# Deformable convolution: adding the bilinear corners pairwise on VectorE, through PSUM, ahead of the transposes

## The chip, the core and the metric

The kernel runs on one core of a Trainium2 chip. The metric is device time in microseconds for one launch on the whole input (four images). A core has a TensorE for matrix products and transposes, VectorE and ScalarE for element-wise work, GpSimd, which here also issues the gathers, SyncE for other transfers, and the memories SBUF and PSUM. In the profile they are PE (with PEld, its weight loads), DVE, ACT, POOL and SP.

## The reference, cut to what matters

Four layers act on x of shape 4 x 56 x 56 x 128: a window-attention block, a state-space block (selective scan), a deformable 3 x 3 convolution and a second window-attention block; each is applied to a group-normalised x and added to it. The change lies in the third layer:

```python
offsets = lax.conv_general_dilated(x, offset_w, ...) + offset_b       # 9 taps x (dy, dx)
py = row + ky + dy;  px = col + kx + dx
y0, x0 = floor(py), floor(px);  wy, wx = py - y0, px - x0
val = gather(y0i, x0i) * ((1 - wy) * (1 - wx))[..., None] + gather(y0i, x0i + 1) * ((1 - wy) * wx)[..., None] \
    + gather(y0i + 1, x0i) * (wy * (1 - wx))[..., None] + gather(y0i + 1, x0i + 1) * (wy * wx)[..., None]
out = jnp.einsum('bhwkc,kcf->bhwf', val, kernel.reshape(KK, C, F)) + bias
```

For each of the 3136 positions of an image and each of 9 taps, four corner vectors of 128 channels are weighted and summed, and the 9 sums are multiplied with a 128 x 128 matrix each.

## The kernel before, in words

The images go one after the other through the four layers. The residual image x stays in SBUF, channels on the partitions.

`deform` first normalises x, writes into a table in DRAM, for each position, the four corner vectors of its cell side by side (512 floats a row), computes the offsets, the row numbers (`idx`) and the four corner weights (`wts`, which lie in PSUM, two banks). Then comes the part that the change touches, in a schedule written out by hand: each engine executes its own instructions in the order in which the loop below names them, and waits only for data and for free buffers.

The 3136 positions are 28 tiles of 112 positions (`QB`), four tiles (`nq`) to a column block of 448 (`CH`), seven blocks to an image. For each tile t:

- `gather(t)` (L1298): nine indirect DMAs, one per tap, issued by GpSimd; each fetches 112 table rows, positions on the partitions, into the buffer `g` of the tile. There are four such buffers, so the gathers of tile t wait until the transposes of tile t-4 have released theirs.
- `weigh(t)` (L1307): three VectorE products in place, each over three taps and four corners, 1,536 elements per partition. I call three taps of a tile a third.
- `turn(t)` (L1318): the patches must be turned so that channels lie on the partitions. For each tap, TensorE transposes the four corner blocks one after the other into the same PSUM columns and adds them there, which also sums the four corners. Three taps fill a PSUM tile (`pvt`, four buffers), which ScalarE copies to SBUF (L1319) into `turned`. That is 36 transposes and three copies per tile, 4032 and 336 in all.
- After `turn` of tile 4(c+1), or at the very end for the last block, `product(c)` (L1325): nine products of 128 x 128 by 128 x 448 summed in PSUM (`pdo`, 18 matmul records), then on VectorE the addition of bias and residual (L1327) and the statistics of the next normalisation (L115).

The order matters in one place: VectorE meets the addition of block c after the weighing of tile 4(c+1) and before that of tile 4(c+1)+1, so it stands there until TensorE has the product. The next layer starts when the last addition and its statistics are done, since its normalisation needs the whole image.

Of the kernel before, what the change touches and what calls it, by code (L numbers as in the profile page):

```python
# [10 lines left out]
F32 = mybir.dt.float32  # L11
# [3 lines left out]
ALU = mybir.AluOpType  # L15
# [4 lines left out]
P = 128  # L20
# [15 lines left out]
QB = 112  # L36
NTB = L // QB
# [12 lines left out]
KK = 9  # L50
# [28 lines left out]
class _Net:  # L79
# [1123 lines left out]
    def deform(self, b, x):  # L1203
# [3 lines left out]
        nc, tc, w = self.nc, self.tc, self.w["L2"]  # L1207
# [3 lines left out]
        with tc.tile_pool(name="df", bufs=1) as s1, tc.tile_pool(name="df_ps", bufs=1, space=PSUM) as s1x, tc.manual_schedule():  # L1211
# [3 lines left out]
            wts = [wps[:QB, i, :nw].rearrange("q (n k) -> q n k", k=4) for i in range(2)]  # L1215
            with tc.tile_pool(name="dc", bufs=1) as sb, tc.tile_pool(name="dc_ps", bufs=6, space=PSUM) as ps:
# [7 lines left out]
                for c in range(NCK):  # L1224
                    cols = slice(c * CH, (c + 1) * CH)
                    self.gn_apply(xg[:, cols], x[:, cols], gn)
                    pt = bank("pgt")
                    for i in range(nq):
                        t = c * nq + i
                        nc.tensor.transpose(pt[:QB, i * P : (i + 1) * P], xg[:, t * QB : (t + 1) * QB], self.ident)  # L1230
                    nc.scalar.copy(gt[:, c * nq : (c + 1) * nq, :].rearrange("q t c -> q (t c)"), pt[:QB, :])
                    if c in (3, NCK - 1):
                        ts = slice(0 if c == 3 else 4 * nq, (c + 1) * nq)
                        for k in range(4):
                            for r in range(2):

                                y = r + 1 - k // 2
# [9 lines left out]
                for g in range(2):  # L1247
                    n = min(4, NCK - 4 * g)
                    pf = bank("pf")
                    for k in range(KK):  # L1250
                        ky, kx = k // 3, k % 3
                        for j in range(n):
                            c = 4 * g + j
                            nc.tensor.matmul(
                                pf[32 * j : 32 * j + 32, :CH].rearrange("p (h w) -> p h w", w=HW),
                                lhsT=w["offset_w"][:, k * 32 : (k + 1) * 32],
                                rhs=gp[:, 8 * c + ky : 8 * c + ky + 8, kx : kx + HW],
                                start=(k == 0),
                                stop=(k == KK - 1),
                            )  # L1260
                    nc.scalar.activation(of[: 32 * n, g, :], pf[: 32 * n, :CH], AF.Identity, bias=w["offset_b"][: 32 * n, :])
                for g in range(2):
                    n = min(4, NCK - 4 * g)
                    pt = bank("pof")
# [27 lines left out]
            with tc.tile_pool(name="dg", bufs=2) as sb, tc.tile_pool(name="dg_ps", bufs=2, space=PSUM) as ps:  # L1292
                patch, turned = {}, {}

                def gather(t):
                    patch[t] = sb.tile([QB, KK, 4 * P], F32, tag="g", name="g", bufs=4)
                    for k in range(KK):
                        nc.gpsimd.indirect_dma_start(  # L1298
                            out=patch[t][:, k], out_offset=None, in_=tab[:, :],
                            in_offset=bass.IndirectOffsetOnAxis(ap=idx[:, t * KK + k : t * KK + k + 1], axis=0),  # L1300
                        )

                def weigh(t):
                    g = patch[t].rearrange("q k (s c) -> q (k s) c", s=4)
                    wv = wts[2 * t // NTB][:, t % (NTB // 2) * KK : (t % (NTB // 2) + 1) * KK, :].rearrange("q k s -> q (k s)")
                    for k in range(0, 4 * KK, 12):
                        nc.vector.tensor_tensor(g[:, k : k + 12], g[:, k : k + 12], wv[:, k : k + 12, None].to_broadcast([QB, 12, P]), ALU.mult)  # L1307

                def turn(t):
                    c, i = divmod(t, nq)  # L1310
                    if i == 0:
                        turned[c] = sb.tile([P, KK, CH], F32, tag="vt", name="vt")
                    g = patch.pop(t)
                    for k in range(0, KK, 3):
                        pt = ps.tile([P, 3, QB], F32, tag="tr", name="pvt", bufs=4)
                        for m in range(3):
                            for s in range(4):
                                nc.tensor.matmul(pt[:, m, :], lhsT=g[:, k + m, s * P : (s + 1) * P], rhs=self.ident[:QB, :QB], start=(s == 0), stop=(s == 3), is_transpose=True)  # L1318
                        nc.scalar.copy(turned[c][:, k : k + 3, i * QB : (i + 1) * QB], pt)  # L1319

                def product(c):
                    vt = turned.pop(c)
                    po = ps.tile([P, 512], F32, tag="y", name="pdo")
                    for k in range(KK):
                        nc.tensor.matmul(po[:, :CH], lhsT=w["kernel"][:, k * P : (k + 1) * P], rhs=vt[:, k, :], start=(k == 0), stop=(k == KK - 1))  # L1325
                    cols = slice(c * CH, (c + 1) * CH)
                    nc.vector.scalar_tensor_tensor(x[:, cols], po[:, :CH], w["bias"], x[:, cols], ALU.add, ALU.add)  # L1327
                    self.stats(x, c)

                for t in range(NTB + 1):  # L1330
                    if t < NTB:
                        gather(t)
                        weigh(t)
                        turn(t)

                    if t >= nq and t % nq == 0 and t < NTB:
                        product(t // nq - 1)
                product(NCK - 1)

    def finish(self, b, x, cols):  # L1340
# [108 lines left out]
```

## Time and profile before

| | |
|---|---|
| median of three runs | 13576.5 us (13573.9 to 13580.56) |
| the profiled execution's own time | 13561.7 us |
| its span, first to last instruction | 13559.6 us |
| busy: PE, PEld | 12015.1 us (89%), 7682.4 us (57%) |
| busy: DVE, ACT, POOL | 9310.6 us (69%), 7569.9 us (56%), 9553.4 us (70%) |
| first stage, first gather to last addition | 381.30 us (2157.09 to 2538.39) |
| busy in it: PE, PEld, DVE, ACT, POOL | 221.72, 168.99, 149.65, 35.46, 235.71 us |
| in it: granted TensorE clock, share of the DMA engines | 0.69, 0.54 |

The span lies in one profiled execution; the 2.1 us between it and that execution's time lie around it. The shares of the whole span mix four layers with different limits, so the rows of the stage count here. There are four such stages, one per image. A line of the profile names the kernel's line, the engine, the operation, the output and input by the program's names and the count; "idle before" is how long the engine had stood, and "<-" what ended it. "issue" means that the profile shows nothing it waited for; "remote" that it can't name the releaser.

### The profile page before, as it was taken

The page shows a single profiled execution, that of the slowest core. Times are in us where ns is not written, and L with a number is a line of the kernel's source. Part 1 is how long each engine was busy: PE and PEld are TensorE (multiplying, and loading weights), DVE is VectorE, ACT ScalarE, POOL GpSimd, SP SyncE. Part 2 cuts the span into 40 slices and gives each one's busy share as a digit, 9 for nine tenths or more (in the row PEclk, how much of TensorE's full clock was granted, in tenths as well). Part 3 has the DMA queues.
Part 4 walks back from the last instruction along what each step waited for, and adds up shares of the span by engine and source line. Part 5 has one row for each costly group of instructions (what it writes and reads, how often), then busy time and mean ns, then how long its engine had stood idle before and what let it go on. Part 6 is the DMA issues. An engine that isn't in the chain of part 4 may idle for free. (4 is left out here: it accounts for less than half of the span.)

```text
span 13559.6 us, 223295 instructions
## 1 busy us (share of the span) xinstructions
PE 12015.1 (89%) x88500; PEld 7682.4 (57%) x88500; DVE 9310.6 (69%) x11503; ACT 7569.9 (56%) x19306; POOL 9553.4 (70%) x6660
## 2 busy tenths in 40 slices
PE   8989995799998999579999899957999989995799
PEld 4448883544544888354444488845444448884544
DVE  6649993565665999356467499944656659994564
ACT  5567761356556776135655677613565567761356
POOL 4849994477484999448748499943874849994386
PEclk9999997899999999789999899978999999997899
DMA  2000004200000000420000000042000000004200
GB/s 97 1 13 5 4 4 123 68 1 8 4 1 13 5 4 4 126 65 1 8 4 1 13 5 4 4 126 64 1 9 3 1 13 5 4 4 128 62 1 6
DMA packets 181196, 344.93 MB, mean 25 GB/s; under 512 B 20104, under 2 KB 101416, under 8 KB 180024
## 3 DMA queue, kind: packets, MB, share of 16 engines
q0 software_dynamic: 80640, 231.28, 6.1%
q1 hardware_dynamic: 99224, 97.83, 2.3%
q8 instruction: 700, 11.47, 0.4%
q14 instruction: 344, 2.82, 0.1%
q10 hardware_dynamic: 288, 1.53, 0.0%
HBM read 256.04 MB, written 74.52 MB: 24 GB/s over the span
## 5 line engine op out<-in xcount | busy, mean ns | idle before, releaser
L545 POOL TENSOR_TENSOR es<-es,e 128x896 f32<-128x896 f32 x1824 | 3768.0, 2089 | 483.2 <-ACT e L539 440.5
L347 DVE TENSOR_REDUCE mx<-pm 128x1 f32<-128x512 f32 (+2 forms) x4928 | 3060.0, 671 | 1321.4 <-PE pm L346 715.8
L539 ACT ACTIVATE e<-pst 128x448 f32<-128x448 f32 (+1 forms) x5600 | 2675.6, 544 | 1993.4 <-PE pst L537 1405.7
L1056 DVE TENSOR_TENSOR_SCAN hs<-da,dbu 128x928 f32<-128x928 f32 x1792 | 3633.0, 2070 | 53.4 <-ACT dbu L1049 29.0
L1065 POOL TENSOR_TENSOR hs<-hs,cb 128x896 f32<-128x896 f32 x1792 | 3463.4, 1943 | 26.0 <-ACT carry L1060 20.4
L346 PE MATMUL pm<-ks,qs 32*128 32x512 f32 (+1 forms) x9856 | 2886.2, 634 | 14.1 <-DVE nm L363 8.5
L537 PE MATMUL pst<-qs,ks 32*128 32x448 f32 x11200 | 2680.9, 547 | 0.0
L1074 PE MATMUL yt<-w_C,hs 128*116 128x128 f32 x14336 | 1865.5, 273 | 1.1 <-POOL hs L1065 1.1
L532 PE MATMUL pst<-nm,sel 32*128 32x448 f32 x5600 | 1615.5, 612 | 0.0
L1074 PEld LDWEIGHTS yt<-w_C,hs 128*116 128x116 f32 x14336 | 1570.3, 135 | 2.1 <-POOL hs L1065 2.1
L1038 PE MATMUL dbu<-dgb,ut 112*128 112x224 f32 x7168 | 1257.5, 298 | 270.0 <-DVE hs L1056 269.9
L1298 POOL DMA_INDIRECT g<-tab,idx x1008 | 940.2, 933 | 626.9 <-issue 432.5
L561 PE MATMUL po<-e,va 128*32 128x448 f32 (+1 forms) x11200 | 1350.8, 551 | 0.0
L346 PEld LDWEIGHTS pm<-ks,qs 32*128 32x128 f32 x9856 | 909.7, 185 | 741.7 <-DVE mx L347 592.1
L1318 PE MATMUL pvt<-w_C,g 112*128 112x112 f32 x4032 | 652.8, 321 | 710.0 <-issue 603.9
L1038 PEld LDWEIGHTS dbu<-dgb,ut 112*128 112x128 f32 x7168 | 944.4, 192 | 535.5 <-DVE hs L1056 525.6
L992 ACT ACTIVATE da<-dl,A 128x112 f32<-128x112 f32 x3584 | 1194.5, 383 | 0.1
L537 PEld LDWEIGHTS pst<-qs,ks 32*128 32x128 f32 x11200 | 1101.3, 184 | 105.6 <-issue 19.2
L1318 PEld LDWEIGHTS pvt<-w_C,g 112*128 112x128 f32 x4032 | 555.3, 178 | 817.0 <-issue 795.8
L532 PEld LDWEIGHTS pst<-nm,sel 32*128 32x128 f32 x5600 | 558.1, 184 | 751.2 <-DVE mx L347 378.6
L1319 ACT COPY vt<-pvt 128x336 f32<-128x336 f32 x336 | 142.0, 440 | 1413.2 <-remote 921.8
L1060 ACT COPY carry<-hs 128x32 f32<-128x32 f32 x1792 | 397.6, 222 | 624.4 <-DVE hs L1056 616.3
(228 smaller groups left out, 15590.6 us busy)
## 6 DMA issues: line engine op xcount, KB each, us to landing
tab<-zero SPq DMA_DIRECT2D x4, 6728.0 KB
g<-tab,idx POOLq DMA_INDIRECT x1008
tab<-gt SPq DMA_DIRECT2D x32, 448.0 KB
dl_d<-dl SPq DMA_DIRECT2D x28, 448.0 KB
dl<-dl_d SPq DMA_DIRECT2D x56, 224.0 KB
tab<-gt SPq DMA_DIRECT2D x32, 336.0 KB
out_dram<-x SPq DMA_DIRECT2D x28, 224.0 KB
x<-in_x_dram SPq DMA_DIRECT2D x21, 224.0 KB
```

The source lines that it names most:

```text
L346: nc.tensor.matmul(pm[:, :m], lhsT=qs[head(h), q.start : q.start + P], rhs=ks[head(h), keys], start=True, stop=True)
L347: nc.vector.tensor_reduce(mx[:n, h, kc : kc + 1], pm[:n, :m], AX.X, ALU.max)
L532: nc.tensor.matmul(t[:, :CH], lhsT=self.sel[head(h), :], rhs=nm[head(h), part(qc)], start=True, stop=False)
L537: nc.tensor.matmul(t[:, :CH], lhsT=ks[head(h), k * KB : (k + 1) * KB], rhs=qs[head(h), part(qc)], start=False, stop=True)
L539: nc.scalar.activation(e[:nk, j, :], t[:nk, :CH], AF.Exp, scale=SCALE)
L545: nc.gpsimd.tensor_tensor(s, es[g - 1, p][:nk] if k == 1 else s, e[:nk], ALU.add)
L561: nc.tensor.matmul(m["po"][head(h), :CH], lhsT=va[:nk, k, head(h)], rhs=src(h)[:nk], start=(k == 0), stop=(k == NKB - 1))
L1038: nc.tensor.matmul(pu[:, 8 * h : 8 * h + 8, 2 + tb * TB : 2 + (tb + 1) * TB], lhsT=made[g]["ut", 2 * r + tb][:, d, :], rhs=made["r", g // ...
L1056: nc.vector.tensor_tensor_scan(flat(pairs[u // 2][:, d % 2]), flat(made[g]["da"][:, r]), flat(banks.pop(u)), 0.0, ALU.mult, ALU.add)
L1065: nc.gpsimd.tensor_tensor(hs, hs, made["r", g // 2]["cb"][:, :, r * HW : (r + 1) * HW], ALU.mult)
L1074: nc.tensor.matmul(sums[q][:YR, e * P : (e + 1) * P], lhsT=hs[:, n, :], rhs=self.ident, start=(n == 0), stop=(n == NST // 2 - 1), is_trans ...
L1318: nc.tensor.matmul(pt[:, m, :], lhsT=g[:, k + m, s * P : (s + 1) * P], rhs=self.ident[:QB, :QB], start=(s == 0), stop=(s == 3), is_transpo ...
```

## The change

The corners lie in the order (top left, top right, bottom left, bottom right) as four blocks of 128 channels. `weigh` now takes each third in three instructions instead of one: it multiplies the last two corners (`far`) with their weights into a new PSUM tile `pa` (two banks, one buffer), multiplies the first two in place, and adds `far` to them in place. Two blocks remain per tap, so `turn` transposes and sums two instead of four: 18 transposes a tile. To make room in PSUM, the transposing tile `pvt` has three buffers instead of four, and the product's tile `pdo` one instead of two. Each `far` product waits for the sum before it, whose input it overwrites, and each sum for the product just before it. Gathers, copies, products and their order are as they were.

```diff
                 def weigh(t):
-                    g = patch[t].rearrange("q k (s c) -> q (k s) c", s=4)
-                    wv = wts[2 * t // NTB][:, t % (NTB // 2) * KK : (t % (NTB // 2) + 1) * KK, :].rearrange("q k s -> q (k s)")
-                    for k in range(0, 4 * KK, 12):
-                        nc.vector.tensor_tensor(g[:, k : k + 12], g[:, k : k + 12], wv[:, k : k + 12, None].to_broadcast([QB, 12, P]), ALU.mult)
+
+                    g = patch[t].rearrange("q k (s c) -> q k s c", s=4)
+                    wv = wts[2 * t // NTB][:, t % (NTB // 2) * KK : (t % (NTB // 2) + 1) * KK, :, None].to_broadcast([QB, KK, 4, P])
+                    for k in range(0, KK, 3):
+                        ks = slice(k, k + 3)
+                        pa = ps.tile([P, 2, 512], F32, tag="pa", name="pa", bufs=1)
+                        far = pa[:QB].rearrange("q a b -> q (a b)")[:, : 6 * P].rearrange("q (k s c) -> q k s c", k=3, s=2)
+                        nc.vector.tensor_tensor(far, g[:, ks, 2:, :], wv[:, ks, 2:, :], ALU.mult)
+                        nc.vector.tensor_tensor(g[:, ks, :2, :], g[:, ks, :2, :], wv[:, ks, :2, :], ALU.mult)
+                        nc.vector.tensor_tensor(g[:, ks, :2, :], g[:, ks, :2, :], far, ALU.add)
 
                 def turn(t):
...
                     for k in range(0, KK, 3):
-                        pt = ps.tile([P, 3, QB], F32, tag="tr", name="pvt", bufs=4)
+                        pt = ps.tile([P, 3, QB], F32, tag="tr", name="pvt", bufs=3)
                         for m in range(3):
-                            for s in range(4):
-                                nc.tensor.matmul(pt[:, m, :], lhsT=g[:, k + m, s * P : (s + 1) * P], rhs=self.ident[:QB, :QB], start=(s == 0), stop=(s == 3), is_transpose=True)
+                            for s in range(2):
+                                nc.tensor.matmul(pt[:, m, :], lhsT=g[:, k + m, s * P : (s + 1) * P], rhs=self.ident[:QB, :QB], start=(s == 0), stop=(s == 1), is_transpose=True)
                         nc.scalar.copy(turned[c][:, k : k + 3, i * QB : (i + 1) * QB], pt)
 
                 def product(c):
                     vt = turned.pop(c)
-                    po = ps.tile([P, 512], F32, tag="y", name="pdo")
+                    po = ps.tile([P, 512], F32, tag="y", name="pdo", bufs=1)
```

## The prediction

> **What bounds the kernel now.** I read the groups of the page first, then the waits and the timeline of one deformable stage, the only place the diff touches. In the groups, columns are busy time and mean, then idle time before and what ended it:
>
> ```profile
> L1298 POOL DMA_INDIRECT g<-tab,idx x1008 | 940.2, 933 | 626.9 <-issue 432.5
> L1318 PE MATMUL pvt<-w_C,g 112*128 112x112 f32 x4032 | 652.8, 321 | 710.0 <-issue 603.9
> L1319 ACT COPY vt<-pvt 128x336 f32<-128x336 f32 x336 | 142.0, 440 | 1413.2 <-remote 921.8
> ```
>
> No engine is full in this stage: TensorE idles as long as it works, waiting for nothing the profile names. The timeline of VectorE shows the shape of the stage, first image:
>
> ```profile
> 2255.38 0.69 DVE L1327 SCALAR_TENSOR_TENSOR x<-pdo,w_L,x 128x448 f32<-128x448 f32 x1 [38.44 <-PE pdo L1325]
> 2256.10 0.63 DVE L115 BATCH_NORM_STATS2 gn_st<-x 128x6 f32<-128x448 f32 x1
> 2256.65 20.05 DVE L1307 TENSOR_TENSOR g<-g,wt 112x1536 f32<-112x1536 f32 x12
> 2307.51 0.68 DVE L1327 SCALAR_TENSOR_TENSOR x<-pdo,w_L,x 128x448 f32<-128x448 f32 x1 [30.81 <-PE pdo L1325]
> ...
> 2513.13 0.68 DVE L1327 SCALAR_TENSOR_TENSOR x<-pdo,w_L,x 128x448 f32<-128x448 f32 x1 [30.19 <-PE pdo L1325]
> 2513.85 0.63 DVE L115 BATCH_NORM_STATS2 gn_st<-x 128x6 f32<-128x448 f32 x1
> 2514.39 15.05 DVE L1307 TENSOR_TENSOR g<-g,wt 112x1536 f32<-112x1536 f32 x9
> 2537.71 0.68 DVE L1327 SCALAR_TENSOR_TENSOR x<-pdo,w_L,x 128x448 f32<-128x448 f32 x1 [8.26 <-PE pdo L1325]
> ```
>
> From the first gather at 2157.09 the stage is an opening of 98.3 us to the first addition, five rounds of four tiles each (257.75 us, 51.5 each), a tail of 24.6 and the last addition of 0.7: 381.3 us. In every round VectorE weighs 12 thirds of a tile in 20 us and then stands about 30 us until the product is there. So VectorE has room, and the round is set elsewhere. GpSimd's timeline:
>
> ```profile
> 2239.39 0.93 POOL L1298 DMA_INDIRECT g<-tab,idx  x1 [0.30 <-issue]
> 2240.63 0.93 POOL L1298 DMA_INDIRECT g<-tab,idx  x1 [0.30 <-issue]
> 2245.32 0.93 POOL L1298 DMA_INDIRECT g<-tab,idx  x1 [3.76 <-remote]
> ```
>
> A gather costs 1.237 us, the 36 of a round 44.5 us. Twice a round one waits about 3.5 us longer: 44.5 + 2 x 3.5 = 51.5, the whole round. What it waits for is a buffer that TensorE has not released. TensorE and ScalarE in the first gathers:
>
> ```profile
> 2191.30 0.35 PE L1318 MATMUL pvt<-w_C,g 112*128 112x112 f32 x1 [1.65 <-issue]
> 2194.09 0.35 PE L1318 MATMUL pvt<-w_C,g 112*128 112x112 f32 x1 [2.44 <-issue]
> 2196.89 0.35 PE L1318 MATMUL pvt<-w_C,g 112*128 112x112 f32 x1 [2.45 <-issue]
> ```
> ```profile
> 2182.91 0.44 ACT L1319 COPY vt<-pvt 128x336 f32<-128x336 f32 x1 [7.57 <-PE pvt L1318]
> 2212.30 0.44 ACT L1319 COPY vt<-pvt 128x336 f32<-128x336 f32 x1 [28.95 <-remote]
> 2219.37 1.34 ACT L1319 COPY vt<-pvt 128x336 f32<-128x336 f32 x3 [6.63 <-remote]
> ```
>
> The transposes for the copy at 2212.30 are drawn at 2180 to 2182.6; their copy came 30 us later, just after the last gather before the long pause (2211.72). While gathers flow, TensorE finishes a first batch promptly and then trickles: 12 matmuls and 12 weight loads from 2190 to 2219 us, 0.86 instructions per us. In a pause it catches up within about 4.4 us. I don't know what holds it, only that it goes with gathers in flight.
>
> **What the skill says.** The Trainium skill, Perfetto Trace Analysis, "Summary: the profiler window per engine type": a TensorE end is estimated. The 30 us between drawn end and copy agree, so I date completions by the copies. PSUM — Partial Sum Buffer, "Engine vs sequencer instructions": TensorE's queue is 64 deep and matmuls complete in order; the trace agrees in kind, late completions holding all behind them. SBUF — State Buffer, "Who interferes with whom": a VectorE instruction with at most one SBUF input doesn't contend with GpSimd. The gathers keep 1.237 us while VectorE weighs; all three new operations keep one input in PSUM, so I charge them nothing there.
>
> **The change, step by step.**
> VectorE. A third was one product of 1,536 elements, 1748 ns: 148 above 1536/0.96. VectorE: DVE Perf Modes, "The TRN2 errata", gives (N+151)/0.96, so 1757, which agrees. The new 768-element product I put at 800 + 148 = 948 ns. In a burst, thirds follow each other every 1664 ns, 84 less than one lasts. Now the far product waits for the previous sum, the near one waits for nothing new, and the sum waits for the near product, at 30 ns per wait (addition end to statistics above): 948 + 864 + 30 + 948 + 30 = 2.82 us a third, not 1.66. No row writes 768 elements to PSUM or reads both kinds so; bounds 2.6 and 3.4. Behind the far product's wait queue all later thirds, the addition and the statistics; TensorE waits for them, then GpSimd through the buffers.
> What hides it: 12 thirds take 33.8 us; with 1.3 for addition and statistics, 0.7 for the last turn, 7 to 9 for the product and 0.6 to the next addition, VectorE's loop is 43.4 to 45.4 us, about GpSimd's 44.5. The cover is just enough in the rounds; at 3.4 us a third it is gone. In the tail there is none: nine thirds cost 25.4 instead of 15.05, less 0.7 for half a turn: 24.6 + 10.3 - 0.7 = 34.2 us.
> TensorE. A third falls from 12 pairs and a semaphore wait (25 instructions) to 6 pairs and one (13). A round falls from 12 x 25 + 36 for the product = 336 to 192. Two pauses cleared 336, 168 each, of which 22 trickled in 25.7 us and 146 came in a burst. Then 192 = 146 n + 0.86 x 48, n = 1.03. Three transposing buffers instead of four let less work queue up, and pauses don't come when the product wants them, so I take 1.3 pauses: 44.5 + 1.3 x 3.5 = 49.0 us. Ends: 46 (no pause, VectorE's loop) and 54.
> The single product buffer waits for an addition over 40 us back: nothing.
> Opening. The first weighing of tile 4 ends at 2218; unhindered, product and addition would follow at 72 us. But 15 x 13 + 36 = 231 instructions exceed the burst at the start (100 by 2183 us) plus the trickle; the gathers of tiles 7 and 8 come at 78 and 89 us, and the pause there frees the product, which ends at 92 or 103. I take 95, against 98.3.
> Sum: 95 + 5 x 49.0 + 34.2 + 0.7 = 374.9 us against 381.3, so 6.4 less, 26 in four images. The profiled execution's own time is 13561.7 us (span 13559.6), which becomes 13536; the median is 14.8 higher: 13550 us.
>
> **The rivals.**
> The product is caught. With fewer instructions all four buffered tiles are released in time, so no pause is due when the product's 36 instructions meet the trickle; 36/0.86 is 42 us instead of 9. VectorE stands at the addition until GpSimd, four tiles ahead, pauses too. I estimate 17 us more in every second round: (61.5 + 46)/2 = 54 us. 95 + 270 + 34.9 = 399.9, 18.6 more, 13651 us. It decides from an average round of 50.3 us on. For it: the late completions above. Against: products now run in 7 to 9 us, just after pauses.
> TensorE keeps up wholly: opening 72, rounds 46: 72 + 230 + 34.9 = 336.9, 44.4 less, 13399 us. For it: fewer than half the transposes are needed per pause; against: 192 is still over 146.
> VectorE becomes the bound: at 3.3 us a third its loop is 50.3 us and the tail 38.5: 95 + 251.5 + 39.2 = 385.7, 4.4 more, 13594 us. Against it: the formula fits today's product within 0.5%.
>
> **How the numbers follow.** Forecast 0.40 (own range 13500 to 13600), product caught 0.30, TensorE free 0.15, VectorE bound 0.15. About 0.2%, 27 us, can be told from no change. The forecast gives 0.22 faster, 0.14 same, 0.04 slower; the caught product 0.03 same, 0.27 slower; TensorE free 0.15 faster; VectorE bound 0.02, 0.06, 0.07. Together 0.39, 0.23, 0.38. The range 13430 to 13650 leaves about a tenth on each side.
>
> **What would show it.** Three VectorE groups of 336, each near 950 ns; 2016 transposes; a tail near 34 us; rounds near 49 us with one or two pauses. A round above 51 us with idle VectorE before the addition is the caught product; one with no idle VectorE is the third rival; 46 us without pauses the second. Gathers slower than 1.237 us would make all of it wrong.

## The result, and the profile after

The changed kernel takes 13685.15 us (median of four runs, 13657.67 to 13689.08), the kernel before 13575.2 (four runs, 13558.07 to 13580.56): a ratio of 1.0079, 95% interval 1.0061 to 1.0096. It is slower, by 0.8%, and outside the predicted range. The profiled execution took 13687.81 us, its span is 13686.0, 126.4 more than before. The four deformable stages, first gather to last addition, take 413.05, 399.74, 404.15 and 413.26 us against 381.3, 381.0, 381.5 and 381.4: 104.9 of the 126.4. The other 21.5 lie outside the stages, where the code is the same. That part of the span ranges from 12031.9 to 12070.1 us over the profiled executions of this study, before and after included, so I don't put it down to the change.

The groups of the kernel after that touch the stage; columns as before, busy and mean, then idle time before and what ended it:

```profile
L1298 POOL DMA_INDIRECT g<-tab,idx x1008 | 941.3, 934 | 681.3 <-issue 438.4 <-PE pvt L1324 125.1 <-remote 114.5
L1324 PE MATMUL pvt<-w_C,g 112*128 112x112 f32 x2016 | 438.9, 392 | 1017.7 <-issue 807.0 <-DVE g L1313 113.9 <-ACT vt L1325 96.7
...
L1311 DVE TENSOR_TENSOR pa<-g,wt 112x768 f32<-112x768 f32 x336 | 322.7, 961 | 112.2 <-DMA g<-tab,idx 101.6 <-issue 1.1 <-DVE g L1313 0.8
L1313 DVE TENSOR_TENSOR g<-g,pa 112x768 f32<-112x768 f32 x336 | 320.5, 954 | 11.5
L1312 DVE TENSOR_TENSOR g<-g,wt 112x768 f32<-112x768 f32 x336 | 318.2, 947 | 0.0
```

The work is what the diff says. The transposes' busy time falls from 652.8 to 438.9 us and VectorE's rises from 566.4 to 961.4. But TensorE's idle time in front of the transposes grows from 710.0 to 1017.7 (807.0 of it "issue", with nothing in the profile that it waits for), and GpSimd's in front of the gathers from 626.9 to 681.3. Of the latter, 125.1 us now end with a transpose that releases a patch buffer ("<-PE pvt"), against 10.6 before.

VectorE's timeline, first image, the additions and one third between them:

```profile
2244.56 0.68 DVE L1333 SCALAR_TENSOR_TENSOR x<-pdo,w_L,x 128x448 f32<-128x448 f32 x1 [27.27 <-PE pdo L1331]
2245.28 0.63 DVE L115 BATCH_NORM_STATS2 gn_st<-x 128x6 f32<-128x448 f32 x1
2245.82 0.94 DVE L1311 TENSOR_TENSOR pa<-g,wt 112x768 f32<-112x768 f32 x1
2246.68 0.95 DVE L1312 TENSOR_TENSOR g<-g,wt 112x768 f32<-112x768 f32 x1
2247.66 0.95 DVE L1313 TENSOR_TENSOR g<-g,pa 112x768 f32<-112x768 f32 x1
2248.65 0.96 DVE L1311 TENSOR_TENSOR pa<-g,wt 112x768 f32<-112x768 f32 x1
...
2278.92 0.95 DVE L1313 TENSOR_TENSOR g<-g,pa 112x768 f32<-112x768 f32 x1
2320.71 0.68 DVE L1333 SCALAR_TENSOR_TENSOR x<-pdo,w_L,x 128x448 f32<-128x448 f32 x1 [40.84 <-remote]
...
2367.86 0.68 DVE L1333 SCALAR_TENSOR_TENSOR x<-pdo,w_L,x 128x448 f32<-128x448 f32 x1 [11.85 <-issue]
...
2484.44 0.68 DVE L1333 SCALAR_TENSOR_TENSOR x<-pdo,w_L,x 128x448 f32<-128x448 f32 x1 [27.65 <-remote]
2531.65 0.68 DVE L1333 SCALAR_TENSOR_TENSOR x<-pdo,w_L,x 128x448 f32<-128x448 f32 x1 [11.90 <-PE pdo L1331]
2568.84 0.68 DVE L1333 SCALAR_TENSOR_TENSOR x<-pdo,w_L,x 128x448 f32<-128x448 f32 x1 [10.40 <-PE pdo L1331]
```

A third takes 2.83 us (2245.82 to 2248.65). The five rounds are 76.1, 47.2, 53.6, 63.0 and 47.2 us long. Where VectorE stands 11 to 12 us at the addition, the round is 47; where it stands 41, it is 76. What TensorE and then GpSimd do in that longest stand:

```profile
2279.97 0.77 PE L1324 MATMUL pvt<-w_C,g 112*128 112x112 f32 x6 [2.08 <-issue]
2280.57 8.64 PE L1331 MATMUL pdo<-vt,w_L 128*128 128x448 f32 x18
2324.86 1.35 PE L1324 MATMUL pvt<-w_C,g 112*128 112x112 f32 x6 [35.64 <-issue]
```
```profile
2312.19 0.93 POOL L1298 DMA_INDIRECT g<-tab,idx  x1 [0.30 <-issue]
2313.42 0.93 POOL L1298 DMA_INDIRECT g<-tab,idx  x1 [0.30 <-issue]
2332.17 0.94 POOL L1298 DMA_INDIRECT g<-tab,idx  x1 [17.81 <-PE pvt L1324]
```

The product's matmuls are drawn at 2280.6 to 2289.2, yet the addition that needs them starts at 2320.7. GpSimd gathers on until 2313.42, when it has filled all four patch buffers and must wait for one. Only 7.3 us after that last gather does the addition start. Then VectorE weighs the next tile, TensorE turns it, and the buffer comes free at 2332.17: a pause of 17.5 us beyond the usual spacing, where before none inside the rounds exceeded 3.7. This is the course that the prediction's rival "the product is caught" describes.

### The profile page after: what moved, and what is told of

It reads as the page before. It is cut to its first block, busy times and chain, and to the rows that moved or that the text cites. A ratio compares the mean times of both kernels' runs of the same rounds, so it can differ in the third digit from the quotient of the medians.

```text
span 13686.0 us, 220239 instructions
## 1 busy us (share of the span) xinstructions
PE 11836.4 (86%) x86484; PEld 7484.2 (55%) x86484; DVE 9676.1 (71%) x12175; ACT 7576.5 (55%) x19306; POOL 9555.8 (70%) x6660
## 5 line engine op out<-in xcount | busy, mean ns | idle before, releaser
L1056 DVE TENSOR_TENSOR_SCAN hs<-da,dbu 128x928 f32<-128x928 f32 x1792 | 3633.0, 2070 | 53.6 <-ACT dbu L1049 29.5
L1298 POOL DMA_INDIRECT g<-tab,idx x1008 | 941.3, 934 | 681.3 <-issue 438.4
L1324 PE MATMUL pvt<-w_C,g 112*128 112x112 f32 x2016 | 438.9, 392 | 1017.7 <-issue 807.0
L1324 PEld LDWEIGHTS pvt<-w_C,g 112*128 112x128 f32 x2016 | 343.5, 218 | 1122.0 <-issue 850.1
```

Of the source, the lines that this page charges most:

```text
L1056: nc.vector.tensor_tensor_scan(flat(pairs[u // 2][:, d % 2]), flat(made[g]["da"][:, r]), flat(banks.pop(u)), 0.0, ALU.mult, ALU.add)
```

## The experiments

One thing has to be said ahead. The runs fall into groups 1 to 9, each on one chip with the kernel before beside it. In some groups TensorE doesn't trickle at all, for a reason that stays open: it ran free in five (kernel before 13349.7 to 13377.2 us) and trickled as in the first profiles in four (13566.1 to 13572.5). The profiles of one group agree on it. So each row of the table is compared with the kernel before of its own group. A profile of group 1, with only the buffer counts changed, shows TensorE in the middle of flowing gathers:

```profile
2186.01 2.47 PE L1318 MATMUL pvt<-w_C,g 112*128 112x112 f32 x12 [1.16 <-ACT vt L1319]
2189.84 2.47 PE L1318 MATMUL pvt<-w_C,g 112*128 112x112 f32 x12 [1.35 <-ACT vt L1319]
```

Twelve transposes in 2.47 us, where the prediction's profile had one each 2.8 us. No gather waits, the rounds are GpSimd's own (44.7 us on average, 36 gathers of 1.241 us each), and a stage is 327.7 us on average instead of 381.3. Below, such a TensorE is called free.

| group | kernel | before, us | this, us | ratio (95%) | stages, us |
|---|---|---|---|---|---|
| 1, free | near product only | 13377.24 | 13363.29 | 0.9986 (0.9977 to 0.9995) | 325.7 to 326.4 |
| 1, free | four transposes again | 13377.24 | 13417.15 | 1.0031 (1.0020 to 1.0043) | 338.6 to 340.0 |
| 1, free | buffers only | 13377.24 | 13379.62 | 1.0001 (0.9992 to 1.0010) | 327.3 to 328.6 |
| 1, free | late addition | 13377.24 | 13375.46 | 0.9998 (0.9989 to 1.0006) | 327.6 to 328.4 |
| 2, free | after | 13356.16 | 13384.05 | 1.0023 (1.0015 to 1.0031) | 330.1 to 333.0 |
| 2, free | late addition | 13356.16 | 13352.19 | 0.9997 (0.9990 to 1.0004) | 327.1 to 328.2 |
| 2, free | three patch buffers | 13356.16 | 13382.33 | 1.0019 (1.0012 to 1.0027) | 330.6 to 332.6 |
| 2, free | no gathers | 13356.16 | 13372.72 | one run | 329.9 to 330.8 |
| 3, free | after | 13371.78 | 13384.4 | 1.0010 (1.0003 to 1.0018) | 330.6 to 332.7 |
| 3, free | late addition | 13371.78 | 13368.44 | 0.9998 (0.9988 to 1.0008) | 327.3 to 328.3 |
| 4, trickling | late addition | 13572.45 | 13505.61 | one run | 367.4 to 369.1 |
| 5, free | before, late addition | 13349.73 | 13354.87 | one run | 326.9 to 328.3 |
| 5, free | three patch buffers | 13349.73 | 13395.55 | one run | 331.7 to 332.9 |
| 6, free | three patch buffers | 13363.31 | 13400.7 | one run | 331.5 to 332.9 |
| 7, trickling | near product only | 13566.83 | 13619.75 | one run | 388.9 to 397.6 |
| 8, trickling | before, late addition | 13566.06 | 13555.3 | one run | 374.1 to 375.3 |
| 8, trickling | three patch buffers | 13566.06 | 13620.3 | one run | 391.1 to 399.3 |
| 9, trickling | late addition | 13572.25 | 13531.75 | 0.9966 (0.9952 to 0.9979) | 367.6 to 369.2 |

The theories I went in with: the caught product, and against it that VectorE's longer chain of three waiting instructions sets the round.

### The parts alone (group 1)

Near product only: the halved transposes with a short VectorE chain. The far corners are left out.

```diff
-                        nc.vector.tensor_tensor(far, g[:, ks, 2:, :], wv[:, ks, 2:, :], ALU.mult)
                         nc.vector.tensor_tensor(g[:, ks, :2, :], g[:, ks, :2, :], wv[:, ks, :2, :], ALU.mult)
-                        nc.vector.tensor_tensor(g[:, ks, :2, :], g[:, ks, :2, :], far, ALU.add)
```

> Leaves out the two bottom corners: VectorE only weighs the two top ones in place, one product of 768 elements a third, and TensorE transposes two blocks per tap, with the buffers of the changed kernel. So it is the halving of the transposes alone, with less VectorE work than before. Theory of the caught product (TensorE finishes late while gathers flow; with half the transposes the gathers no longer pause before the product, and VectorE stands at the addition): rounds still of two kinds, about 47 us and above 60 us, VectorE idle 20 to 45 us before the long additions, GpSimd with single pauses above 10 us; the time about 13575 us (13530 to 13640) although both engines have less to do. Theory that the longer VectorE chain cost the time: rounds of 46 us, one stage near 320 us, 13330 us. Theory that the fewer PSUM buffers did it: as the first, slower than before.

Four transposes again: the long VectorE chain, with TensorE turning each of the two blocks twice, so that the sums come out doubled.

```diff
-                            for s in range(2):
-                                nc.tensor.matmul(pt[:, m, :], lhsT=g[:, k + m, s * P : (s + 1) * P], rhs=self.ident[:QB, :QB], start=(s == 0), stop=(s == 1), is_transpose=True)
+                            for s in range(4):
+                                nc.tensor.matmul(pt[:, m, :], lhsT=g[:, k + m, (s % 2) * P : (s % 2 + 1) * P], rhs=self.ident[:QB, :QB], start=(s == 0), stop=(s == 3), is_transpose=True)
```

> VectorE as in the changed kernel (three operations a third), but TensorE transposes four blocks per tap again, each of the two sums twice, so the sampled values are doubled; buffers as in the changed kernel. It is the VectorE part alone. Caught product: the pauses come early again, rounds near 52 us without the 60 to 76 us ones, opening near 98, tail 36 to 37, so about 13.5 us more than before per image: 13630 us (13600 to 13660), below the changed kernel. Longer VectorE chain: as slow as the changed kernel or slower, 13685 to 13720 us. Fewer buffers: 13685 us.

Buffers only: the kernel before with the smaller PSUM pools.

```diff
-                        pt = ps.tile([P, 3, QB], F32, tag="tr", name="pvt", bufs=4)
+                        pt = ps.tile([P, 3, QB], F32, tag="tr", name="pvt", bufs=3)
...
-                    po = ps.tile([P, 512], F32, tag="y", name="pdo")
+                    po = ps.tile([P, 512], F32, tag="y", name="pdo", bufs=1)
```

> The kernel before with three transposing buffers and one product buffer. Caught product and longer VectorE chain: no difference that counts, 13575 us within 25, rounds near 51.5 us. Fewer PSUM buffers: most of the loss appears, 13650 us or more.

Late addition: the kernel after, with VectorE's addition taken three tiles later, so that VectorE doesn't stand in front of the product; the last block's comes at the very end.

```diff
                 def product(c):
...
+                    done[c] = po
+
+                def add(c):
+                    po = done.pop(c)
                     cols = slice(c * CH, (c + 1) * CH)
                     nc.vector.scalar_tensor_tensor(x[:, cols], po[:, :CH], w["bias"], x[:, cols], ALU.add, ALU.add)
...
                         weigh(t)
+                        if t >= nq + 3 and (t - 3) % nq == 0:
+                            add((t - 3) // nq - 1)
                         turn(t)
```

> The changed kernel with the addition of a block and its statistics moved three tiles later in VectorE's order (after the weighing of tile 4(c+1)+3 instead of 4(c+1)); nothing is left out. Caught product: VectorE no longer stands at the addition, so a late product costs nothing until 22 us and more; rounds fall to 47 to 49 us, the single pauses above 10 us vanish, one stage is 345 to 360 us, 13450 us (13410 to 13520). Longer VectorE chain: VectorE's work is the same, so at most the idle time of a few us per round goes: 13640 us or more. Fewer buffers: 13650 us or more.

All four expectations stood on a trickling TensorE, and none could be tested: it ran free. What the group does give is the price of the parts where TensorE is free. Halved transposes together with half of VectorE's products earn 0.14%, fewer buffers cost nothing measurable, VectorE's chain with TensorE's old work costs 0.31%: rounds of 45.1 to 46.7 and a tail of 37 to 38 us where the run with only the buffers changed has 44.7 and 33.4 on average.

### The kernel after again, and its two neighbours (groups 2 and 3)

> The kernel after, unchanged, timed again. In the profile first shown TensorE trickled at 0.86 instructions per us while gathers flowed; in the first four experiments it did not, and a gather never waited. If it trickles here, the product is caught again: rounds of 47 and 53 to 76 us, stages of 400 to 413 us, ratio to before about 1.008. If TensorE runs free here, VectorE sets the round: 12 thirds of 2.84, 2.0 for addition and statistics and turn, and 9.5 to 11 us from the last weighing to the addition (the idle time of VectorE there in the run with only the buffers changed, 9.7 to 11.3) give 45.6 to 47 us against 44.5 before, and the tail grows by 3 us, so a stage of about 338 against 327.4 and a ratio of 1.002 to 1.003. If in the free case the halved transposes decided instead, the ratio would be below 1.000.

> The kernel after with VectorE's addition taken three tiles later, timed again beside the kernel after. Caught product (TensorE trickling): VectorE no longer stands behind the product, so no idle time of over 15 us before the addition, and a ratio to before of 0.99 (13450 where before takes 13575). Long VectorE chain: no better than the kernel after. TensorE free: again a stage of 328 us in rounds of 44.5, ratio 1.000, that is 0.002 to 0.003 under the kernel after, because the 9.5 to 11 us at the addition are taken out of VectorE's loop.

Three patch buffers: the kernel after, with GpSimd able to run only three tiles ahead.

```diff
-                    patch[t] = sb.tile([QB, KK, 4 * P], F32, tag="g", name="g", bufs=4)
+                    patch[t] = sb.tile([QB, KK, 4 * P], F32, tag="g", name="g", bufs=3)
```

> The kernel after with three patch buffers instead of four, so that GpSimd can be only three tiles ahead. Caught product (TensorE trickling): VectorE stands until GpSimd runs out of buffers, which is now one tile, 11 us, earlier; the idle times before the caught additions, 41 us in the profile of after, come down to about 30, and the ratio falls from 1.008 to about 1.004. Rival (the stall is set by the number of instructions TensorE has left): as long as before or longer, 1.008 or more. TensorE free: GpSimd may wait for buffers while VectorE stands 10 us at the addition, so 1.002 to 1.006.

No gathers: tiles from the fourth on use the first four patches again.

```diff
+                    if t >= 4:
+                        patch[t] = kept[t % 4]
+                        return
-                    patch[t] = sb.tile([QB, KK, 4 * P], F32, tag="g", name="g", bufs=4)
+                    patch[t] = kept[t] = sb.tile([QB, KK, 4 * P], F32, tag="g", name="g", bufs=4)
```

> The kernel after, but only the first four patches of each image are gathered; all later tiles weigh and turn those four again, so the deformable stages compute something else and GpSimd does nothing in their rounds. If the gathers are what holds TensorE, it never trickles here, and the round is VectorE's own loop: 45.6 to 47 us in all rounds. If something else holds TensorE, rounds above 50 us remain. If GpSimd's 44.5 us set the round of the kernel after where TensorE is free, the rounds fall below 44 here.

> The kernel after once more, to see whether TensorE trickles here. Two chips have shown it free, with a ratio of 1.0023. Trickling: before near 13575 us, stages of 400 to 413 us, ratio 1.008. Free: before near 13360 us, stages of 330 to 333 us in rounds of 44.4 to 45, ratio 1.002.

> The addition three tiles later, beside the kernel after. Trickling: the caught product no longer holds VectorE, no idle time over 15 us before an addition, ratio to before 0.99; if the long VectorE chain were the cause, no better than the kernel after. Free: 328 us a stage and ratio 1.000, as on two chips before.

VectorE's timeline of the kernel after in group 2, and its gathers as a group:

```profile
2270.25 0.69 DVE L1333 SCALAR_TENSOR_TENSOR x<-pdo,w_L,x 128x448 f32<-128x448 f32 x1 [9.71 <-PE pdo L1331]
2314.94 0.68 DVE L1333 SCALAR_TENSOR_TENSOR x<-pdo,w_L,x 128x448 f32<-128x448 f32 x1 [9.40 <-PE pdo L1331]
2359.47 0.68 DVE L1333 SCALAR_TENSOR_TENSOR x<-pdo,w_L,x 128x448 f32<-128x448 f32 x1 [9.24 <-PE pdo L1331]
```
```profile
L1298 POOL DMA_INDIRECT g<-tab,idx x1008 | 940.4, 933 | 454.0 <-issue 434.7 <-DMA g<-tab,idx 13.4 <-DVE g L1313 3.7
```

Where TensorE is free, no product is caught: VectorE stands 9 to 10 us for the product itself, and the rounds are 44.4 to 46.7, most of them shorter than the 45.6 to 47 I expected; the stages are 331.7 us on average, not about 338. The change then costs 0.1 to 0.2%. Without gathers the rounds stay at 44.4 to 46.1: the expectation of less than 44 fails, and so does that of 45.6 to 47 in all rounds. It is thus VectorE's own loop, with the stand in it, that sets these rounds, and it is about as long as the 44.5 us of GpSimd's 36 gathers; it lies within the prediction's 43.4 to 45.4 but for the longest.

The stages are 4.1 us longer than with only the buffers changed (group 1), 3.3 of which are the tail (36.7 against 33.4 us, over the last gaps between additions). Nine thirds of the longer chain cost 10.4 us more; in the tail of the kernel with only the buffers changed VectorE waits for gathers instead (6.0 us in the first image), so less than that is seen. The late addition takes even the 3.3 away. A buffer less for the patches costs nothing more here (1.0019 against 1.0023). As TensorE was free in this group, the run cannot say whether the gathers are what holds TensorE.

### Where TensorE trickles (groups 4, 7, 8 and 9)

> One look at the kernel with the addition three tiles later, for a chip on which TensorE trickles. Trickling: the kernel before takes about 13575 us here, and this one 13450 if the caught product is what cost the kernel after its time (VectorE never stands over 15 us before an addition), or 13650 and more if the long VectorE chain is. Free: before near 13365, this one the same, 328 us a stage.

VectorE's timeline of that run, the additions of the first image in two pieces:

```profile
2364.22 0.68 DVE L1337 SCALAR_TENSOR_TENSOR x<-pdo,w_L,x 128x448 f32<-128x448 f32 x1
...
2424.46 0.68 DVE L1337 SCALAR_TENSOR_TENSOR x<-pdo,w_L,x 128x448 f32<-128x448 f32 x1 [12.33 <-remote]
2463.11 0.68 DVE L1337 SCALAR_TENSOR_TENSOR x<-pdo,w_L,x 128x448 f32<-128x448 f32 x1
...
2525.58 0.69 DVE L1337 SCALAR_TENSOR_TENSOR x<-pdo,w_L,x 128x448 f32<-128x448 f32 x1 [6.53 <-PE pdo L1331]
```

The work on every engine is that of the kernel after; only the place of the additions and their statistics in VectorE's order differs. The stage falls from 407.5 us on average in the kernel after to 368.0. VectorE's chain is as long as there, so the theory that the long chain by itself set the round falls. I had put the gain at 125 us on before, and it was 66.8: no stand before an addition is longer than 12.7 us, but GpSimd still pauses, 42.2 us in the first image, close to the 45.2 of the kernel before.

> The near product alone with halved transposes, so the far half of each patch is left out: VectorE's chain is as short as before, TensorE's work that of the kernel after. Trickling chip (before near 13572): if fewer transposes catch the product by themselves, rounds of over 60 us with VectorE idle before the addition remain, 13600 or more; if it takes VectorE's longer chain as well, it is faster than before, below 13540. Free chip: 0.9986 again.

The halved transposes with the short chain, VectorE and GpSimd:

```profile
2372.32 0.68 DVE L1329 SCALAR_TENSOR_TENSOR x<-pdo,w_L,x 128x448 f32<-128x448 f32 x1 [52.36 <-remote]
2373.04 0.63 DVE L115 BATCH_NORM_STATS2 gn_st<-x 128x6 f32<-128x448 f32 x1
2373.58 10.45 DVE L1309 TENSOR_TENSOR g<-g,wt 112x768 f32<-112x768 f32 x12
2429.29 0.68 DVE L1329 SCALAR_TENSOR_TENSOR x<-pdo,w_L,x 128x448 f32<-128x448 f32 x1 [45.26 <-remote]
...
2486.10 0.68 DVE L1329 SCALAR_TENSOR_TENSOR x<-pdo,w_L,x 128x448 f32<-128x448 f32 x1 [45.10 <-remote]
```
```profile
2364.92 0.93 POOL L1298 DMA_INDIRECT g<-tab,idx  x1 [0.30 <-issue]
2378.48 0.93 POOL L1298 DMA_INDIRECT g<-tab,idx  x1 [12.63 <-PE pvt L1320]
```

This is the caught product in its pure form. VectorE works 12 us of a 56.9 us round and stands 45; GpSimd pauses once a round, 12.3 us, and 44.5 + 12.3 = 56.8. The product whose addition starts at 2372.32 is drawn from 2329.78 on; the addition comes 7.4 us after the last gather before the pause. VectorE has less to do than in the kernel before and the kernel is 0.4% slower (one run of each): the product is caught without VectorE's longer chain.

One difference besides the halved transposes is left: this kernel, like the kernel after, has three transposing buffers and one product buffer. Alone they cost nothing where TensorE is free (1.0001); where it trickles they were not run alone. The late addition has them too, and its rounds are no longer than those of the kernel before (51.2 against 51.5 us on average), so they don't cost the time by themselves; whether the product would also be caught with the four and two of before is not shown. VectorE's long chain with four transposes was not run there either.

The pause also shows where the 17.5 us of the kernel after come from. Both begin with 7.3 to 7.4 us until the product is through; then three thirds must be weighed before a buffer is turned free, 2.6 us here and 8.5 there, and 17.5 - 12.3 = 5.2 is about that difference of 5.9.

> The kernel before (one VectorE operation a third, four transposes) with VectorE's addition three tiles later. Trickling chip (before near 13572): in before the product is caught at no addition, and VectorE stands about 30 us at each while GpSimd waits twice a round for TensorE. If the gain of the late addition over the kernel after (13505 against about 13685) came from not standing at a caught product alone, it changes little here, 13550 to 13575. If VectorE's standing at the addition in itself holds up TensorE's next tiles, it gains here too: down to 13510. Free chip: the same as before within 0.1%.

> The kernel before with the addition three tiles later, for a chip on which TensorE trickles (kernel before near 13570 there). If only a caught product makes VectorE's place at the addition cost time, it gains little, 13550 to 13575; if VectorE's 30 us stand at each addition of the kernel before costs by itself, 13510 or less. Free chip: within 0.1% of before.

The same edit in the kernel before. Trickling, its rounds stay at 51.5 us on average with the addition late, and 6.6 us a stage go from opening and tail; the time of one run falls by 10.8 us, 0.08%. A stand of 30 us at each addition, as in the kernel before, costs next to nothing in the rounds. Free, no change.

> The kernel after with three patch buffers, for a chip on which TensorE trickles (before near 13572). Caught product ended by GpSimd running out of buffers: idle times before the caught additions of about 30 us instead of 41, and 13630 where the kernel after takes 13685. Stall set by TensorE's own backlog: 13685 or more. Free chip: 1.002 again, as measured on another chip.

> The kernel after with three patch buffers, once more in search of a chip on which TensorE trickles (before near 13572). Caught product ended by GpSimd running out of buffers: idle times before the caught additions of about 30 us instead of 41, and 13630 where the kernel after takes 13685. Stall set by TensorE's own backlog: 13685 or more. Free chip: 1.002 to 1.003 again.

> The kernel after with three patch buffers, for a chip on which TensorE trickles. Stall ended by GpSimd running out of buffers: about 30 us idle before the caught additions, 13630. Ended by TensorE's own backlog: 41 us, 13685 or more. Free chip: 1.002 to 1.003.

Two of the three met a free TensorE (0.3% over before each, one run). The third met a trickling one; VectorE and GpSimd, first image:

```profile
2306.14 0.68 DVE L1333 SCALAR_TENSOR_TENSOR x<-pdo,w_L,x 128x448 f32<-128x448 f32 x1 [34.64 <-remote]
...
2407.00 0.68 DVE L1333 SCALAR_TENSOR_TENSOR x<-pdo,w_L,x 128x448 f32<-128x448 f32 x1 [18.89 <-remote]
2469.36 0.69 DVE L1333 SCALAR_TENSOR_TENSOR x<-pdo,w_L,x 128x448 f32<-128x448 f32 x1 [27.05 <-remote]
```
```profile
2302.19 0.93 POOL L1298 DMA_INDIRECT g<-tab,idx  x1 [0.30 <-issue]
2317.61 0.93 POOL L1298 DMA_INDIRECT g<-tab,idx  x1 [14.48 <-PE pvt L1324]
```

Taking a buffer away makes the kernel faster than the kernel after: 13620.3 us (0.40% over its before, one run of each) where the kernel after was 0.79% over. In the first image the long pause comes after gather 108 instead of 117, one tile sooner, and the longest stand is 34.6 instead of 40.8, with four stages 47.8 us shorter in all. The direction and the total are as the caught product wants it (13630 expected), but in part by luck: the single stand shrank by 6 us, not 11, and the rounds did not get shorter (56.0 us on average against 55.0). The gain lies in the openings, 78.0 us on average against 94.6, where VectorE stands 15.4 to 19.7 us before the first addition instead of 26.7 to 51.3. So this run shows that the long stand ends sooner when GpSimd runs out of buffers sooner, but not that a round gets cheaper by it.

> The kernel after with the addition three tiles later, timed for an interval where TensorE trickles. One look there gave 13505.6 against 13572.5 for the kernel before, 0.9951. Trickling: 0.994 to 0.996. Free chip: 0.9997 to 1.0000, as on three chips.

The late addition timed: 0.9966, interval 0.9952 to 0.9979, a little less than the single run promised. This version beats the kernel after where both ran in one group (0.9997 against 1.0023, 0.9998 against 1.0010) and by their ratios where TensorE trickles (0.9966 against 1.0079). It beats the kernel before by 0.3% where TensorE trickles and equals it where TensorE is free.

## Why the prediction was wrong

**VectorE.** The cost was right. A third is 2.83 us (2.82 forecast), its instructions 961, 947 and 954 ns (948). The Trainium skill, VectorE: DVE Perf Modes, "The TRN2 errata", gives (768 + 151)/0.96 = 957, which agrees. No contention shows either: a gather takes 934 ns against 933 before, as the skill's SBUF — State Buffer, "Who interferes with whom", let me assume for operations with one operand in PSUM.

**Opening.** 95 forecast; 88.1, 112.2, 90.7 and 87.5 measured, 94.6 on average. That the average fits is luck: three images lie 4 to 8 us below the forecast, and the second lies 17 above it, because there the first product is caught and VectorE stands 51.3 us.

**Tail.** 34.2 forecast, 37.0 measured on average. Nine thirds take 25.5 us, as foreseen (25.4); VectorE then stands 10.4 us for the last product in the first image, not the 8.26 - 0.7 that the forecast left for it.

**Rounds: here it failed.** "192 = 146 n + 0.86 x 48, n = 1.03 ... so I take 1.3 pauses: 44.5 + 1.3 x 3.5 = 49.0 us" forecast 49.0; the average is 55.0. In the rounds of the four images GpSimd pauses 1.6 times a round for 6.1 us on average, 9.8 us a round, where the forecast had 1.3 pauses of 3.5 us, 4.5 a round; this is most of the difference. So the step that failed is the price of a pause, 3.5 us taken over from the kernel before, more than their number.

The balance counts how much catching up TensorE needs and lets pauses come as needed. It leaves out when they come and what has to happen before they end. GpSimd's pauses are set by the release of buffers four tiles back. As I read the timelines, with half the work TensorE releases all of these in one pause, so the next pause is late, and the product, issued in between, meets the trickle. VectorE stands behind it; nothing is weighed; GpSimd fills its lead; and the pause that follows must wait for the product, the weighing and the turning of a tile. The first stage has nine pauses of 63.6 us together where the kernel before had twelve of 45.2: fewer, as the balance said, but the longest is 17.5 us, five times as long. The late addition shows the price wrong once more: with 192 instructions a round and no long stand, there are 1.35 pauses a round, as forecast, but of 4.9 us, and rounds still average 51.2 us in group 4, not 49.0. Why these pauses are longer than 3.5 us is left open.

**The sum.** 94.6 + 5 x 55.0 + 37.0 + 0.7 = 407.3, against 374.9 forecast and 407.5 measured.

**The rivals.** "The product is caught" is what happened, with a chance of 0.30 beside the forecast's 0.40. It said 54 us a round and 399.9 a stage. Its argument against itself, that products run in 7 to 9 us just after pauses, described the kernel before, where, as I read it, TensorE's own backlog put the product there; the change took that away. "TensorE keeps up wholly" gave 336.9 us a stage, against a kernel before at 381.3. Where TensorE is free, the stages of the kernel after are 331.7 and 331.9 on average, but those of the kernel before, with only its buffers or its addition changed, are 327 to 329: there is nothing to gain, which that rival missed. "VectorE becomes the bound" had thirds of 3.3 us and rounds of 50.3, and neither came. But where TensorE is free VectorE's loop of 44.4 to 46.1 us does set the round, and it leaves nothing to gain.

**The base.** Every step stood on a trickle I couldn't explain and took for a property of the kernel on the chip. In five of the nine groups it was absent, and in the two of these where the kernel after was timed the change cost 0.1 to 0.2%.

## What to carry to other kernels

An engine that is late on average may still be on time where it counts, because its backlog can decide where the waits fall: before taking work off it, ask which instruction now stands where the catching up used to be, and who waits for that one. Place an in-order engine's wait for a result (here VectorE's addition) several steps after the result is due, if the buffers allow it. This costs a few lines. In the kernel after it was worth 0.1 to 0.3% where TensorE was free and about 1.1% where it trickled (1.0079 to 0.9966, in two groups); in the kernel before, where no product was caught, 0.08% in one run. And don't count the pauses of a producer alone: a pause that has to wait for a chain of consumers (here 17.5 us) is several times as long as one that ends with a release nearly due (3.5).

## What the runs showed of the hardware

TensorE is held while gathers flow in some groups of runs and not in others, with the same kernel: the stages of the kernel after take 407.5 us on average or 331.7, those of the kernel before 381.3 or, with only its buffers or its addition changed, about 328. Held, single transposes are drawn to start 2.79, 2.80, 3.49, 2.10 and 2.80 us apart (profile of before, from 2191.30 on), all near multiples of 0.70; free, twelve run in 2.47 us. It isn't one chip's mark: groups 4 and 5 ran on the same chip, trickling in one and free in the other. It isn't the granted clock of TensorE: 0.69 in the first stage of the kernel before and 0.69 in that of the free run with only the buffers changed; 0.59 and 0.60 for the kernel after. It isn't the gathers' own time: they are issued every 1.24 us in both, and their last packet ends about 3.1 us after the issue in both. It doesn't show in the transfer of TensorE's instructions: those packets of 16 KB took 1.13 us on average in the stages of the kernel before, 1.14 in the free run. And it doesn't reach beyond the stages: the rest of the span is 12031.9 to 12057.4 us in trickling profiles, 12039.2 to 12070.1 in free ones. That it comes with gathers and ends within 7.4 us of the last one before a pause is what the timelines above show; that the gathers cause it was only argued, since the run without gathers met a free TensorE.

One thing separates the two kinds of profile in all 20 of them. Each gather has a semaphore that is counted up 16 times as its data lands. The 13 free profiles hold 16126 to 16128 of the 16128 updates of their 1008 gathers (all 2304 in the run without gathers in the rounds), the 7 trickling ones 3194 to 4038. So the profile gives the gathers a time from issue to landing (the last number, in us) only where TensorE is free. The kernel after in the first measurement, then in group 2:

```profile
g<-tab,idx POOLq DMA_INDIRECT x1008
```
```profile
g<-tab,idx POOLq DMA_INDIRECT x1008, 3.4
```

The updates go missing while TensorE is held: in the first stage of the kernel before, 45 to 48 of them are on record in each 4 us from 2161 to 2169 and 4 to 8 in each from 2181 to 2213, with three or four gathers in each such stretch; the free run with only the buffers changed has 48 to 60 over the same time. This also leaves many waits of the trickling profiles without a name ("remote"). Whether what loses the updates also holds TensorE, or both come from something else, no run shows.

How far a drawn end can be from the use of the result: the product drawn to end at 2289.2 was added at 2320.7, and VectorE had stood since 2279.9 with nothing else to wait for. The Trainium skill, Perfetto Trace Analysis, "Summary: the profiler window per engine type", calls TensorE's end estimated; here the two lie 31 us apart.
